# One image's lower-half columns moved from the prologue into layer 0, and what came with it: other DMA queues, a fourth tile of x, another source of a subtraction

## The chip, the cores and the metric

The kernel runs on one core of a Trainium2 chip. The metric is the device time of one execution in microseconds (us); less is better. Five engines work in parallel, each in its own order: TensorE (PE, with its weight loads as PEld), VectorE (DVE), ScalarE (ACT), GpSimd (POOL) and SyncE (SP), which here only issues DMAs. Data lie in DRAM, in SBUF (on chip, 128 partitions) or in PSUM (where TensorE writes its results).

## The reference

x has the shape 4 x 16 x 256 x 256 (images, channels, rows, columns). Two layers follow each other, each with a group norm ahead (8 groups of 2 channels) and a residual:

```
def _L0_conv_ref(x, conv_w, conv_b):          # on h = _gn(x)
    out = conv3x3(x, conv_w) + conv_b         # 16 -> 16*25 channels
    logits = out.reshape(N, C, 25, H, W)
    weights = softmax(logits, axis=2)
    return einsum('ncuij,ncuij->ncij', unfold5x5(x), weights)

x = x + _L0_conv_ref(_gn(x), conv_w, conv_b)
x = x + _L1_conv_ref(_gn(x), ...)             # silu and a cubic spline of 3x3 patches, as one convolution
```

So layer 0 computes 400 logits at each pixel, and with their softmax weighs the 25 neighbours of the normalized image, channel by channel. Layer 1 applies silu and spline bases to the normalized result and convolves them.

## The kernel before, in words

An image's 256 rows are two halves of 128 (NH = 2, "upper" is half 0). There are three stages.

*The prologue* (about the first 120 us). It loads all eight half images (`load_x`, L415 to L424): image 0 into `held`, which stays, the other six into a pool `xin` of three buffers, so that a load waits until the tile three earlier is done with. For every tile VectorE takes statistics (L534, L536), ScalarE squares it into `xq` (L543, one buffer), TensorE sums the squares (L546), and VectorE takes their maximum (L549), for a bound on the logits; the bound becomes the flag (L589) on which all engines branch (L1112, L1116) to layer 0. The weights of both layers are arranged too: `prepare0`, and `prepare1`, which also stores six small pieces of the silu weights on SP's queue (L513).

*The normalized image h in DRAM.* `normalize` (L264) writes h of one image in two layouts. Rows: ScalarE normalizes to `hsp` (L327), and `put_rows` stores it into `hs` (L288, SP's queue). Columns: ScalarE normalizes to `ht` (L340), TensorE transposes it into `tp`, a PSUM tile (L362), and three copies of the columns are made: `tt` (fp32), `hi` (its value rounded to fp32r) and `lo`, the rest, by a subtraction on VectorE (L370); `put_columns` stores `tt` into `hst` and `hi`, `lo` into `hsl` (L302, three stores of 260 KB for each half, SP's queue). Each column tile has a border element from the neighbouring half. h has 4 quarters of the channels (QC = 4) and 2 blocks of columns in each (QG = 4), so there are 8 blocks for each half.

`normalize` is a generator: each `next` issues a little. Its stores and loads are put off by so many steps (`moves`). For image 0 it is interleaved with the statistics of the other images in the prologue, with `tt` copied by VectorE. For images 1 to 3 it is stepped once in each step of layer 0 (`next(ahead, None)`), with `tt` copied by ScalarE; a block of columns takes six steps.

*Layer 0* (`layer0`, from about 120 to 2060 us). The order is image, half, strip of 32 columns (64 strips), and in a strip eight steps of 4 columns. In a step TensorE multiplies `am` (from `hst`) and `an` (from `hsl`) by the weights (L833, L837) into logits in PSUM; ScalarE takes the exponential into the first half of a tile `e` (L856); GpSimd multiplies it by `u`, rows of `hs`, into the second half (L861); VectorE adds up both, one step later (L700). `e` has four buffers. Once in a strip come the division on VectorE (L720 to L722, with the reciprocal `r` in PSUM) and the subtraction from x on GpSimd (L728). `am` and `an` are loaded two column groups (of two steps) ahead by SP (L648, L658), `u` by L672.

*Layer 1* (`layer1`, from about 2030 us): spline pieces on VectorE and ScalarE (L158 to L169), silu on ScalarE (L973), convolution on TensorE (L1037, L1047), and some copies on GpSimd (L1008, L1065, L1067).

What orders the work: each engine runs its list in the order that the framework's scheduler made in the prologue; in layers 0 and 1 the order is that of the program text (`in_order`). A DMA waits on its queue for what it needs and holds up what is behind it on that queue; a DMA on ScalarE's queue stands in ScalarE's own list.

Of the kernel before, what the change touches and what calls it, by code (L numbers as in the profile page):

```python
# [3 lines left out]

# [7 lines left out]
F32 = mybir.dt.float32  # L12
F32R = mybir.dt.float32r
AF = mybir.ActivationFunctionType
# [20 lines left out]
def conv_preact_kernel(  # L35
# [12 lines left out]
    nc = tc.nc  # L48
    B, C, H, W = x.shape
    G = 8  # L50
    GC = C // G
    P = 128
    NH = H // P
# [3 lines left out]
    PAD = K // 2  # L57
# [3 lines left out]
    SW = 32  # L61
# [199 lines left out]
                    hsl[b][h][:, :, w : w + RP].rearrange("c t r -> (c t) r"), zero[:, 0:RP],  # L261
                )

    def normalize(b, ptr, tiles, held=None, copier=None):  # L264

        prep, xps, tts, his, los = tiles
        copier = copier or nc.scalar.copy

        moves = [(20 + 4 * i, f) for i, f in enumerate(zeros(b, nc.sync))] if held is None else []

        def move():
            for f in [f for i, f in moves if i <= 0]:
                f()
            moves[:] = [(i - 1, f) for i, f in moves if i > 0]

        def load(q, h):
            if held is None and q < C // QC:
                nc.sync.dma_start(  # L280
                    xps[h][:, :, PAD : PAD + W],
                    x[b, q * QC : (q + 1) * QC, h * P : (h + 1) * P, :].rearrange(
                        "c p w -> p c w"),
                )

        def put_rows(q, h, hsp):
            r0 = PAD + h * P
            nc.sync.dma_start(  # L288
                hs[b][:, r0 : r0 + P, q * QC : (q + 1) * QC, :].rearrange(
                    "s r c w -> r s (c w)"),  # L290
                hsp.rearrange("p s c w -> p s (c w)"),
            )

        def put_columns(q, n):
            g0 = n * QG
            for h in range(NH):

                for to, ti, t in ((hst, 0, tts[n]), (hsl, 0, his[n]), (hsl, 1, los[n])):
                    d = to[b][h]
                    m = 2 if to is hsl else 1  # L300
                    t = t if t.dtype == F32 else t.bitcast(F32)
                    nc.sync.dma_start(  # L302
                        bass.AP(
                            tensor=d.tensor,
                            offset=d.offset + q * QC * m * CT + ti * CT + (1 + g0) * RP,
                            ap=[[QW * RP, W // QW], [m * CT, QC], [1, QG * RP]],
                        ),
                        t[:, h].rearrange("p g r -> p (g r)"),
                    )

        def border(t):
            nc.scalar.copy(t[:, 1, :, 0:1], t[:, 0, :, P : P + 1])
            nc.scalar.copy(t[:, 0, :, RP - 1 :], t[:, 1, :, 1:2])

        hts = {}

        def rows(q):
            for h in range(NH):
                xp = xps[h] if held is None else held[h][:, q * QC : (q + 1) * QC]
                hsp = prep.tile([P, NST, QC, SP], F32, name=f"hsp{b}_{q}_{h}", tag="hsp")  # L320
                ht = prep.tile([P, QW, W // QW, QC], F32, name=f"ht{b}_{q}_{h}", tag=f"ht{h}")
                hts[q, h] = ht
                for k in range(QC // GC):
                    g = q * (QC // GC) + k
                    kc = slice(k * GC, (k + 1) * GC)
                    how = dict(scale=nrm[b][:, 0, g : g + 1], bias=nrm[b][:, 1, g : g + 1])
                    nc.scalar.activation(  # L327
                        hsp[:, :, kc, :].rearrange("p s c w -> p c s w"),
                        bass.AP(
                            tensor=xp.tensor, offset=xp.offset + k * GC * (W + 2 * PAD),  # L330
                            ap=[xp.ap[0], [W + 2 * PAD, GC], [SW, NST], [1, SP]],
                        ),
                        AF.Identity, **how,
                    )
                    if k == QC // GC - 1:
                        nc.scalar.copy(hsp[:, 0, :, 0:PAD], zpad)
                        nc.scalar.copy(hsp[:, NST - 1, :, PAD + SW :], zpad)
                        moves.append((4, partial(put_rows, q, h, hsp)))
                    yield
                    nc.scalar.activation(  # L340
                        ht[:, :, :, kc].rearrange("p g w c -> p c w g"),
                        xp[:, kc, PAD : PAD + W].rearrange("p c (w g) -> p c w g", g=QW),
                        AF.Identity, **how,
                    )
                    if k == QC // GC - 1:
                        moves.append((4, partial(load, q + 1, h)))
                    yield

        def columns(q, n, h):

            tp = ptr.tile([P, QG, P], F32, name=f"tp{b}_{q}_{n}_{h}", tag="tp")

            def copy(t, to):

                to(t[:, h, :, 1 : 1 + P], tp)
                if h == 0:
                    to(t[:, 1, :, 0:1], tp[:, :, P - 1 :])
                else:
                    to(t[:, 0, :, RP - 1 :], tp[:, :, 0:1])

            for k in range(QG):
                nc.tensor.transpose(  # L362
                    tp[:, k, :], hts[q, h][:, n * QG + k].rearrange("p w c -> p (w c)"), ident
                )
            yield
            copy(tts[n], copier)
            copy(his[n], nc.scalar.copy)
            yield

            nc.vector.tensor_sub(  # L370
                los[n][:, h, :, 1 : 1 + P], tp, his[n][:, h, :, 1 : 1 + P].bitcast(F32)
            )
            if h == NH - 1:
                moves.append((5, partial(border, los[n])))
                moves.append((9, partial(put_columns, q, n)))
            yield
            yield
            yield
            yield

        for h in range(NH):
            load(0, h)
        yield
        for _ in rows(0):
            move()
            yield
        for q in range(C // QC):
            ahead = rows(q + 1) if q + 1 < C // QC else iter(())
            for n in range(QW // QG):
                for h in range(NH):  # L390
                    for k, _ in enumerate(columns(q, n, h)):
                        if k % 3 == 2:
                            next(ahead, None)
                        move()
                        yield
            for _ in ahead:
                move()
                yield
        while moves:
            move()  # L400
            yield


    with tc.tile_pool(name="prep0", bufs=2) as prep, tc.tile_pool(
        name="pre", bufs=1
    ) as pre, tc.tile_pool(
        name="xin", bufs=3
    ) as xin, tc.tile_pool(name="stat", bufs=2) as stat, tc.tile_pool(
        name="pstat", bufs=1, space=PSUM
    ) as pstat, tc.tile_pool(name="ptr0", bufs=3, space=PSUM) as ptr0:  # L410
# [30 lines left out]
            )  # L441
        for r in (4 * C, 6 * C):
            nc.sync.dma_start(wnr[r : r + 1, :], conv_b)
        nm = 3 * C
        sw = pre.tile([P, 3, 9, nm], F32, name="sw")
        ss = pre.tile([P, 3, 9, nm], F32, name="ss")
# [49 lines left out]
        def prepare1():  # L496
# [10 lines left out]
            for r in range(RT):  # L507
                nc.vector.tensor_copy(
                    wt[:, r : r + 3, :, r, :], wc.rearrange("p d (e o) -> p d e o", e=3)
                )  # L510
                for d in range(3):
                    p = SROWS.index(r + d) * C
                    nc.sync.dma_start(  # L513
                        ws[p : p + C, :, r, :],
                        wb1[d * C : (d + 1) * C].rearrange("p (e o) -> p e o", e=3),
                    )
# [9 lines left out]
        for b in range(B):  # L526
            st = stat.tile([P, G, NH * (GC if b == 0 else 1), 6], F32, name=f"st0_{b}", tag=f"st0{min(b, 1)}")
            for hf in range(NH):
# [19 lines left out]
                    )  # L548
                nc.vector.tensor_reduce(hm[:, n : n + 1], sq, AX.X, ALU.max)  # L549
                next(ahead, None)  # L550
                if n >= NH and n + 3 < B * NH:
                    loaded.append(load_x(n + 3))
            mean, rstd = group_stats(stat, pstat, st, f"x{b}")
            nc.vector.tensor_copy(nrm[b][:, 0], rstd)
            nc.vector.scalar_tensor_tensor(nrm[b][:, 1], mean, -1.0, rstd, ALU.mult, ALU.mult)
# [15 lines left out]
            if b == 1:  # L571
                prepare1()
            if b == 0:
                ahead = normalize(0, ptr0, tiles, held, nc.vector.tensor_copy)
                next(ahead)
        for _ in ahead:
            pass
# [42 lines left out]
    def layer0(shift):  # L620
# [4 lines left out]
        with tc.tile_pool(name=f"prep{arm}", bufs=2) as prep, tc.tile_pool(  # L625
# [172 lines left out]
            for n, (b, hf, s) in enumerate(strips):  # L798
                if (hf, s) == (0, 0):
                    for _ in ahead:  # L800
                        pass
                    ahead = normalize(b + 1, ptr, tiles) if b + 1 < B else iter(())
                    if b == B - 1:
                        bank = ptr.tile([P, QG, P], F32, name=f"ps{arm}", tag="tp")
                        first_scales = [scales(k, partial(lambda k: bank[:, k], k)) for k in range(2)]
                last = (hf, s) == (NH - 1, NST - 1)
                if last:
                    for _ in ahead:
                        pass
                u = us.pop(0)  # L810
                if s * SW % CX == 0:
# [350 lines left out]
```

## Time and profile before

| | |
|---|---|
| median of 3 runs | 3065.07 us (3059.95 to 3065.65) |
| the profiled execution | 3061.86 us, of it span 3059.8 us |
| VectorE busy | 2959.0 us, 97% |
| TensorE busy | 2802.6 us, 92% |
| ScalarE busy | 2236.6 us, 73% |
| GpSimd busy | 1947.6 us, 64% (until layer 1 begins, nearly all) |
| L861, GpSimd, e times u | 512 x 3.54 us |
| L700, VectorE, sums | 512 x 3.48 us |
| L370, VectorE, lo | 64 x 0.68 us: 16 in the prologue, 48 in layer 0 |
| L543, ScalarE, squares | 8 x 3.6 us |
| DMA, mean | 205 GB/s; 276 GB/s over the first 170 us |

How to read it: in a group's line stand the line of the code, the engine, the operation, what it writes and reads, how often, then the busy time and the mean duration, then the engine's idle time before it and what ended that. In a timeline's line stand start and duration. A following instruction's start may lie a little ahead of the end of the one before it on the same engine, so the time from start to start is shorter than the duration.

### The profile page before, as it was taken

Reading aid. Unit: us, or ns where it says so; the run is one execution under the profiler, and the core shown is the slowest. Engines: PE = TensorE matmul, PEld = TensorE weight load, DVE = VectorE, ACT = ScalarE, POOL = GpSimd, SP = SyncE. Lnnn points to the kernel's source line nnn. Section 1 sums busy time; section 2 is a strip of 40 time slices with the busy share of each in tenths; the row PEclk is TensorE's granted clock in tenths of the full one; section 3 lists DMA queues with packets and bytes.
Section 4 is the critical chain, followed back from the end, with each engine's and each line's share of the span. In section 5 each row is a group of like instructions: output and inputs, shape, how many; then the busy total and the mean of one; then the engine's idle time right before and its main releaser. Section 6 shows DMA issues by size and latency. Waiting matters only on the chain.

```text
span 3059.8 us, 39743 instructions
## 1 busy us (share of the span) xinstructions
PE 2802.6 (92%) x14248; PEld 1448.2 (47%) x14248; DVE 2959.0 (97%) x1587; ACT 2236.6 (73%) x2587; POOL 1947.6 (64%) x744
## 2 busy tenths in 40 slices
PE   4499999999999999999999999958999999999998
PEld 3366656656656666666666566632222222222222
DVE  7599999999999999999999999998999999999997
ACT  6466765676766566766646546559999999999996
POOL 4199999999999999999999999980100100000000
PEclk7699999999999999999999999978999999999999
DMA  8988977879878778978767667659999999999994
GB/s 273 290 223 221 258 205 209 222 189 257 234 209 240 196 202 225 248 216 220 212 174 200 164 173 194 161 131 198 201 192 195 198 194 189 198 194 202 190 197 91
DMA packets 350929, 626.29 MB, mean 205 GB/s; under 512 B 41330, under 2 KB 216676, under 8 KB 334852
## 3 DMA queue, kind: packets, MB, share of 16 engines
q1 hardware_dynamic: 318020, 605.29, 81.0%
q10 hardware_dynamic: 30960, 15.73, 1.8%
q0 software_dynamic: 1744, 2.64, 0.3%
q8 instruction: 117, 1.92, 0.3%
q14 instruction: 88, 0.72, 0.1%
HBM read 513.95 MB, written 104.24 MB: 202 GB/s over the span
## 4 chain that ended last, share of the span: by engine, by line
DVE 69%; issue 11%; PE 8%; DMA 3%; ACT 3%; POOL 2%; SPq 1%; DVEq 0%; ACTq 0%; POOLq 0%
DVE nd L700 44%; PE lg L833 6%; DVE ta L168 4%; DVE ta L167 4%; DVE tb L168 4%; DVE tb L167 4%; DVE tb L158 2%; PE lg L837 1%; DVE yo L1020 1%; POOL e L861 1%; DVE r L721 1%; DVE nd L720 1%; DVE lo L370 1%; DMA am<-hst 1%; DVE nd L722 1%
## 5 line engine op out<-in xcount | busy, mean ns | idle before, releaser
L861 POOL TENSOR_TENSOR e<-e,u 128x1600 f32<-128x1600 f32 x512 | 1788.4, 3539 | 49.0 <-ACT e L856 30.9
L833 PE MATMUL lg<-wm,am 128*128 128x400 f32 x4096 | 1734.8, 505 | 83.8 <-ACT e L856 53.0
L700 DVE TENSOR_REDUCE nd<-e 128x128 f32<-128x3200 f32 x512 | 1748.0, 3478 | 29.0 <-POOL e L861 28.9
L837 PE MATMUL lg<-wn,an 97*128 97x400 f32 x2048 | 1344.9, 657 | 17.3 <-DMA an<-hsl 17.3
L856 ACT ACTIVATE e<-lg 128x800 f32<-128x800 f32 x1024 | 818.2, 837 | 708.9 <-DVE nd L700 460.5
L833 PEld LDWEIGHTS lg<-wm,am 128*128 128x128 f32 x4096 | 760.9, 192 | 403.3 <-ACT e L856 98.2
L1037 PE MATMUL yp<-ring,wt 128*32 128x512 f32 x6144 | 745.9, 598 | 87.6 <-DVE ring L169 63.7
L837 PEld LDWEIGHTS lg<-wn,an 97*128 97x128 f32 x2048 | 388.3, 190 | 334.5 <-issue 23.6
L1037 PEld LDWEIGHTS yp<-ring,wt 128*32 128x32 f32 x6144 | 203.7, 109 | 621.7 <-issue 427.7
L954 POOL MEMSET sl<- 16x256 f32 x6 | 1.8, 306 | 402.7 <-ACT ta L163 299.8
L169 DVE SCALAR_TENSOR_TENSOR ring<-ta,ta 128x2048 f32<-128x2048 f32 (+1 forms) x64 | 147.9, 2310 | 2.5
L168 DVE TENSOR_TENSOR ta<-ta,ta 128x2048 f32<-128x2048 f32 (+1 forms) x64 | 147.5, 2305 | 2.8 <-ACT ta L166 2.8
L169 DVE SCALAR_TENSOR_TENSOR ring<-tb,tb 128x2048 f32<-128x2048 f32 x64 | 145.6, 2275 | 2.5
L748 ACT ACTIVATE z<-xc,nrm 128x256 f32<-128x256 f32 x240 | 144.2, 601 | 5.3 <-POOL xc L728 1.2
L168 DVE TENSOR_TENSOR tb<-tb,tb 128x2048 f32<-128x2048 f32 x64 | 145.4, 2271 | 0.0
L1047 PE MATMUL yp<-sl,ws 64*32 64x512 f32 (+1 forms) x1032 | 131.3, 602 | 0.0
L954 POOL MEMSET slc<- 16x256 f32 x2 | 0.6, 307 | 203.1 <-ACT ta L163 203.0
L166 ACT ACTIVATE ta<-ta 128x2048 f32<-128x2048 f32 (+1 forms) x64 | 123.4, 1928 | 2.0
L193 POOL TENSOR_TENSOR d<-d,nrz 128x8 f32<-128x8 f32 x4 | 2.7, 669 | 191.8 <-DVE d L191 191.8
L166 ACT ACTIVATE tb<-tb 128x2048 f32<-128x2048 f32 x64 | 120.6, 1884 | 0.0
L973 ACT ACTIVATE sl<-sl,q 64x2048 f32<-64x2048 f32 x43 | 90.0, 2094 | 1.1
L728 POOL TENSOR_TENSOR xc<-xc,nd 128x512 f32<-128x512 f32 x64 | 82.5, 1289 | 8.2 <-DVE nd L722 8.2
(195 smaller groups left out, 2089.3 us busy)
## 6 DMA issues: line engine op xcount, KB each, us to landing
am<-hst SPq DMA_DIRECT2D x512, 194.6 KB
u<-hs SPq DMA_DIRECT2D x320, 288.0 KB
an<-hsl SPq DMA_DIRECT2D x512, 129.8 KB
xta<-x1s SPq DMA_DIRECT2D x40, 1024.0 KB
xtb<-x1s SPq DMA_DIRECT2D x40, 1024.0 KB
xtc<-x1s SPq DMA_DIRECT2D x40, 1024.0 KB
am<-hst SPq DMA_DIRECT2D x256, 129.8 KB
sl<-x1s SPq DMA_DIRECT2D x166, 128.0 KB
```

Of the source, the lines that this page charges most:

```text
L166: nc.scalar.activation(s1, r1, AF.Square, scale=2.0)
L167: nc.vector.scalar_tensor_tensor(s2, t, 2.0, s2, ALU.subtract, ALU.mult)
L168: nc.vector.tensor_mul(s1, s1, r1)
L169: nc.vector.scalar_tensor_tensor(f, s2, 0.0, s1, ALU.min, ALU.subtract if given else ALU.add)
L700: nc.vector.tensor_reduce(nd[:, :, :, j : j + JG].rearrange("p t c j -> p t j c"), e.rearrange("p t j m c d -> p t j c m d"), AX.XY, ALU.add,)
L748: nc.scalar.activation(z, v, f, scale=nrm[b][:, 0, g : g + 1], bias=nrm[b][:, 1, g : g + 1], accum_out=st1[b][:, t, g, columns_of(n) : col ...
L833: nc.tensor.matmul(lg[:, i, :NL], lhsT=am[:, o : o + P], rhs=wm.rearrange("p m c d -> p (m c d)"), start=True, stop=False,)
L837: nc.tensor.matmul(lg[:, i, :NL], lhsT=an[:, o : o + P], rhs=wn.rearrange("p m c d -> p (m c d)"), start=False, stop=True,)
L856: nc.scalar.activation(ev, lg[:, :, :NL], AF.Exp)
L861: nc.gpsimd.tensor_tensor(e[:, 1].rearrange("p j m c d -> p j (m c) d"), e[:, 0].rearrange("p j m c d -> p j (m c) d"), uv, ALU.mult,)
L1037: nc.tensor.matmul(yp[t * M : (t + 1) * M], lhsT=wt[:, d, e].rearrange("p r o -> p (r o)"), rhs=ring[:, r0 + t * RT + d : r0 + t * RT + d ...
L1047: nc.tensor.matmul(yp[t * M : (t + 1) * M], lhsT=ws[v, e].rearrange("p r o -> p (r o)"), rhs=sl[n % 3][v, t : t + NT + 1 : NT, e : e + W], ...
```

## The change

- In the prologue `normalize` for image 0 gets `part = 0`: it still makes the rows of both halves and transposes both, but of the columns it copies and stores the upper half's alone. Of the lower half it takes the border element, and it keeps the upper half's border elements for later in three small tiles `kept`.
- The lower half's columns are made in layer 0: a second generator, `part = 1`, is chained ahead of image 1's. It loads the lower half of x again (`xp`, 4 loads), makes `ht` on ScalarE, transposes, makes `tt` and `hi` on ScalarE and `lo` on VectorE, and stores. It is finished by the strip numbered 6 at the latest; the lower half's columns are first read for strip 8.
- A block of columns takes four steps instead of six in this generator and in image 1's (`space = 1`).
- The subtraction that makes `lo` reads `tts[n]` (SBUF) where it read `tp` (PSUM), in all four images.
- In the prologue `put_rows` issues on ScalarE's queue instead of SP's, and one step after instead of four.
- The silu weights' six small stores are issued by GpSimd instead of SP.
- `xin` has four buffers instead of three, and the sixth tile of x is loaded ahead of the loop.

```diff
+    NQ = QW // QG
+    kept = [
+        const.tile([P, C // QC * NQ, QG, 1], d, name=f"kept{i}") for i, d in enumerate((F32, F32R, F32R))
+    ]
-    def normalize(b, ptr, tiles, held=None, copier=None):
+    def normalize(b, ptr, tiles, held=None, copier=None, part=None, space=3):
...
+        parts = range(NH) if part is None else (part,)
+        read = range(NH) if part != 1 else (1,)
...
-            nc.sync.dma_start(
+            (nc.sync if held is None else nc.scalar).dma_start(
                 hs[b][:, r0 : r0 + P, q * QC : (q + 1) * QC, :].rearrange(
...
-            for h in range(NH):
+            for h in parts:
 
                 for to, ti, t in ((hst, 0, tts[n]), (hsl, 0, his[n]), (hsl, 1, los[n])):
...
-                        moves.append((4, partial(put_rows, q, h, hsp)))
+                            moves.append((4 if held is None else 1, partial(put_rows, q, h, hsp)))
...
+                if h in parts:
+                    to(t[:, h, :, 1 : 1 + P], tp)
+                if part == 1:
+                    to(t[:, 1, :, 0:1], keep[:, q * NQ + n])
+                elif h == 1:
+                    to(t[:, 0, :, RP - 1 :], tp[:, :, 0:1])
                 else:
-                    to(t[:, 0, :, RP - 1 :], tp[:, :, 0:1])
+                    to(t[:, 1, :, 0:1] if part is None else keep[:, q * NQ + n], tp[:, :, P - 1 :])
...
-            copy(tts[n], copier)
-            copy(his[n], nc.scalar.copy)
+            copy(tts[n], copier, kept[0])
+            copy(his[n], nc.scalar.copy, kept[1])
             yield
+            v = slice(1, 1 + P) if h in parts else slice(RP - 1, RP)
+            to = h if h in parts else 0
             nc.vector.tensor_sub(
-                los[n][:, h, :, 1 : 1 + P], tp, his[n][:, h, :, 1 : 1 + P].bitcast(F32)
+                los[n][:, to, :, v], tts[n][:, to, :, v],
+                his[n][:, to, :, v].bitcast(F32),
             )
...
             yield
+            for _ in range(space):
+                yield
...
-        name="xin", bufs=3
+        name="xin", bufs=4
...
+        loaded.append(load_x(5))
...
-                    nc.sync.dma_start(
+                    nc.gpsimd.dma_start(
                         ws[p : p + C, :, r, :],
...
-                if n >= NH and n + 3 < B * NH:
-                    loaded.append(load_x(n + 3))
+                if n >= NH and n + 4 < B * NH:
+                    loaded.append(load_x(n + 4))
...
-                ahead = normalize(0, ptr0, tiles, held, nc.vector.tensor_copy)
+                ahead = normalize(0, ptr0, tiles, held, nc.vector.tensor_copy, 0)
...
-                    ahead = normalize(b + 1, ptr, tiles) if b + 1 < B else iter(())
+
+                    ahead = normalize(b + 1, ptr, tiles, space=3 if b else 1) if b + 1 < B else iter(())
+                    if b == 0:
+                        late = normalize(0, ptr, tiles, part=1, space=1)
+                        ahead = chain(late, ahead)
...
+                if n == NST - 2:
+                    for _ in late:
+                        pass
```

## The prediction, as it was put on record before the run

> **What bounds the kernel now.** I read the page first: busy shares, slices, chain of waits.
>
> ```profile
> PE 2802.6 (92%) x14248; PEld 1448.2 (47%) x14248; DVE 2959.0 (97%) x1587; ACT 2236.6 (73%) x2587; POOL 1947.6 (64%) x744
> ...
> DVE  7599999999999999999999999998999999999997
> ...
> DVE 69%; issue 11%; PE 8%; DMA 3%; ACT 3%; POOL 2%; SPq 1%; DVEq 0%; ACTq 0%; POOLq 0%
> ```
>
> VectorE (DVE) is full from the third slice (a slice is 76.5 us) to the end; only the first two, the prologue and the start of layer 0, have idle time. So anything that adds to VectorE's time in layer 0 (150 to 2040 us) adds to the total, and anything that shortens the prologue takes off it. Second, the groups of layer 0, in the stretch 160 to 640 us:
>
> ```profile
> L861 POOL TENSOR_TENSOR e<-e,u 128x1600 f32<-128x1600 f32 x131 | 457.7, 3548 | 7.8 <-ACT e L856 5.2 <-DVE nd L700 2.5
> L700 DVE TENSOR_REDUCE nd<-e 128x128 f32<-128x3200 f32 x130 | 444.2, 3478 | 1.0 <-POOL e L861 1.0
> L370 DVE TENSOR_TENSOR lo<-tp,hi 128x512 fp32r<-128x512 f32 x16 | 10.9, 681 | 0.0
> ```
>
> GpSimd (POOL) multiplies e by u almost without a pause (7.8 us idle in 480), VectorE reduces behind it (1.0 us idle). The third line is the subtraction that makes lo: 16 per image. Third, the timeline of one of them:
>
> ```profile
> 448.58 6.87 DVE L700 TENSOR_REDUCE nd<-e 128x128 f32<-128x3200 f32 x2
> 451.51 10.49 POOL L861 TENSOR_TENSOR e<-e,u 128x1600 f32<-128x1600 f32 x3
> ...
> 455.37 0.68 DVE L370 TENSOR_TENSOR lo<-tp,hi 128x512 fp32r<-128x512 f32 x1
> ...
> 455.96 6.87 DVE L700 TENSOR_REDUCE nd<-e 128x128 f32<-128x3200 f32 x2
> ```
>
> It starts in the middle of GpSimd's multiplications and still takes 0.68 us (0.60 from start to next start). One input, tp, lies in PSUM.
>
> Fourth, the one place where VectorE runs operations with two SBUF inputs (L167, L168, L169) while GpSimd reads SBUF, the start of layer 1:
>
> ```profile
> 2047.32 2.55 DVE L167 SCALAR_TENSOR_TENSOR ta<-xta,ta 128x2304 f32<-128x2304 f32 x1
> ...
> 2048.18 1.94 POOL L1065 COPY pad<-edge 128x258 f32<-128x258 f32 x1
> ...
> 2049.79 2.75 DVE L168 TENSOR_TENSOR ta<-ta,ta 128x2304 f32<-128x2304 f32 x1
> 2050.07 2.77 POOL L1067 COPY ring<-edge 128x50 f32<-128x50 f32 x2
> ...
> 2052.57 2.63 DVE L169 SCALAR_TENSOR_TENSOR ring<-ta,ta 128x2304 f32<-128x2304 f32 x1
> 2052.90 2.56 POOL L1008 COPY ring<-pad 128x258 f32<-128x258 f32 x1
> ```
>
> The copy of 128x258 takes 2.56 us here and 0.57 us at its fastest elsewhere (the minimum over L1008's four). L1065 ends at 2050.12, 0.25 us after L167 (2049.87); L1067 at 2052.84 after L168 (2052.54); L1008 at 2055.46 after L169 (2055.20). GpSimd's reads wait for the running VectorE operation and slip in at its end.
>
> [...] 0.68 us for lo beside a busy GpSimd (one SBUF input), 2.56 for 0.57 above. It shows GpSimd waiting for VectorE; the reverse order, VectorE behind a running multiplication, it doesn't show clearly. [...]
>
> **The change part by part.** The profiled execution took 3061.86 us (span 3059.8 and 2.1 around it), 3.2 below the median 3065.07.
>
> (1) *The source of the subtraction.* The diff turns `tp` (PSUM) into `tts[n]` (SBUF) in every call of the normalization; the second input, hi, is in SBUF too. In the built program's order layer 0 holds 56 of these: 3 images x 16 as before, and 8 of the lower half of image 0. All meet GpSimd's stream. For the 48 in the trace I took, at each one's start, what was left of the GpSimd operation then running: 0.05 to 3.51 us, mean 1.72. If VectorE waits for the end of that operation: 56 x 1.72 = +96.3 us. Queued behind it on VectorE are the next reductions; as VectorE has no idle time to give (2.7 us of waiting on GpSimd in all of layer 0), all counts. GpSimd loses 0.6 us per subtraction, 56 x 0.6 = 34 us, but it is the one ahead (two or three tiles of e at the subtraction), so this is hidden unless VectorE's wait is zero. Bounds: 0 (no contention) and 7.4 us each (VectorE gets in only when GpSimd has run out of tiles: the ring holds 4, the lead is 2.36 on average, so 1.72 + 1.64 x 3.485 us from start to start), 56 x 7.4 = 414 us. I take the waiter-gets-in-next reading, as GpSimd does in the last fence.
>
> (2) *Lower half's columns moved.* From the prologue go, per block, a copy on VectorE (0.60 from start to start), a copy on ScalarE (0.48), a subtraction (0.60), 3 stores of 260 KB on SP: eight times that. Layer 0 gets 8 subtractions: 8 x 0.60 = +4.8 us on VectorE. Its ScalarE work (8 ht of 1.1, 16 copies of 0.48, some 0.1 pieces: 20 us over 38 steps of 3.8 us), 32 transposes (0.11 each) and SP's 24 stores and 8 loads (about 0.6 each, 19 us over 145) lie beside engines with room: ScalarE 65% busy, SP issuing 3 us of am and an per 7.6. If that cover failed, a late am would show; bound 0 to 8 us, taken 0. The closer spacing for image 1 (subtractions every 4 reductions instead of 6) is the same work, earlier.
>
> (3) *The prologue's end.* ScalarE's list from 35.34 us on: 16 pairs of hsp and ht at 1.86 = 29.8, 5 squares of x at 3.52 = 17.6, 8 hi copies at 0.48 = 3.8, some 45 small ones at 0.1 = 4.5, weights 2.4: 58 us, so not before 93 without a wait. Before, it ended at 116.45, with 17 us of waits in the timeline. The rows' stores on its queue cost it 8 issues (0.40 each for L782's in layer 0, beside its work). SP loses its wait of 13.7 us at 59 us for hsp, during which the DMA engines fell idle; next late is then ScalarE itself. It meets new waits: its first store of h waits in the built program for the load of a weight (40 to 44 us), hsp buffers have to drain, and the last two squares stand behind everything, with the sum on TensorE between them (xq has one buffer, 3.4 us). Walking the built order of ScalarE, VectorE and SP with these durations, I get the last square to 110, its sum to 113.6, the flag to 116.6 (before: 113.4).
>
> ```profile
> 118.39 0.56 SPq L302 DMA_DIRECT2D hsl<-lo  x1
> 120.44 1.87 SPq L648 DMA_DIRECT2D am<-hst  x3
> ...
> 147.17 0.87 ACT L327 ACTIVATE hsp<-xp,nrm 128x576 f32<-128x576 f32 x1 [11.30 <-DMA am<-hst]
> ...
> 149.56 3.51 POOL L861 TENSOR_TENSOR e<-e,u 128x1600 f32<-128x1600 f32 x1 [9.21 <-ACT e L856]
> ```
>
> SP before issued its last store at 118.4 and the first am at 120.44; after, its stores are out early, and 1.5 us behind the flag gives 118.1: -2.3 us, bounds -15 (half of the waits vanish, x arrives earlier thanks to the fourth tile) and +5. The weights' six small stores (7 us of SP) go to GpSimd, at 0.5 us each (as L569), ahead of wm: about 1 us, hidden.
>
> (4) *Layer 0's start.* ScalarE stops at the first piece that needs xp until 147.17, after two steps' exponentials. In the new order three steps stand ahead of it: one GpSimd step more in the gap, -3.5 us; bounds -6 and 0.
>
> Sum: 96.3 + 4.8 - 2.3 - 3.5 = +95.3, so 3157.2 against the profiled run, 3160 against the median.
>
> **The rivals.** *No lock for this pair* [...]: then 4.8 - 2.3 - 3.5 = -1.0, 3064, not slower. It decides below 0.1 us per subtraction. For it: the trace never shows VectorE waiting like that in layer 0. Against: the fence of layer 1. With the prologue's bounds it spans 3048 to 3075. *Starving:* VectorE gets no turn inside a back-to-back stream: +414, about 3475. For it: L565 took 4.27 us at 37.33 (0.21 its other times) and ended with GpSimd's multiplication L498 at 41.6, having let several GpSimd instructions pass. Against: it is another kind of operation, and GpSimd does get in between VectorE's. *Half paid:* VectorE waits only for part of an operation, 0.5 to 1 us each, 28 to 56 us more than without the lock: 3092 to 3120.
>
> **How the numbers follow.** Forecast 0.50 (3125 to 3215), no lock 0.25 (of it 0.13 faster, 0.08 the same, 0.04 slower), starving 0.17, half paid 0.08. A measurement of this kernel tells about 0.2% (6 us). Faster 0.13, same 0.08, slower 0.79. From 3050 to 3220, starving is left out, and little else; the forecast's own range is 3125 to 3215.
>
> **What would show it.** lo's mean duration in layer 0 well over 0.68 us (about 2.4), ending with GpSimd's e; idle time of GpSimd rising by some 60 us; layer 0 longer by about 100 us while the sum of L700 stays. For step 3, the flag at 113 to 119 us; for step 4, three steps' multiplications ahead of the first ht. Wrong if lo stays at 0.68 us (then the prologue decides), or if it shows 7 us.

## The result, and the profile after

The changed kernel takes 3158.7 us (median of 4 runs, 3150.6 to 3165.9) against 3065.4 for the kernel before (median of 4, 3060.0 to 3069.9): ratio 1.030, 95% interval 1.027 to 1.034. The profiled execution, the fastest of the four, took 3150.6 us, of it span 3148.8: 89.0 more than the span before.

The page of the changed kernel, first: busy shares, the slices of VectorE, the shares of the chain of waits, and three groups (busy time and mean ns, then the idle time ahead and what ended it). L905, L737 and L395 are what was L861, L700 and L370; in the experiments these numbers shift by a line or two.

```profile
PE 2833.5 (90%) x14280; PEld 1460.4 (46%) x14280; DVE 3049.7 (97%) x1587; ACT 2246.2 (71%) x2619; POOL 1978.3 (63%) x750
...
DVE  7499999999999999999999999998999999999997
...
DVE 76%; issue 11%; DMA 4%; PE 3%; POOL 2%; ACT 2%; SPq 1%; DVEq 0%; POOLq 0%; ACTq 0%
...
L905 POOL TENSOR_TENSOR e<-e,u 128x1600 f32<-128x1600 f32 x512 | 1809.3, 3564 | 121.9 <-ACT e L900 95.1
L737 DVE TENSOR_REDUCE nd<-e 128x128 f32<-128x3200 f32 x512 | 1748.2, 3476 | 17.9 <-POOL e L905 17.9
...
L395 DVE TENSOR_TENSOR lo<-tt,hi 128x512 fp32r<-128x512 f32 x72 | 140.1, 1947 | 5.2 <-ACT hi L376 3.0
```

VectorE's share has not changed, 97%, yet it is busy 90.7 us longer. Its main work, the sums of L737, has not grown (1748.0 before). What has grown is the subtraction that makes lo: it did not stand among the costliest groups before and stands there now with 140.1 us. GpSimd's idle time ahead of e has risen from 49.0 to 121.9 us. So an instruction that does the same arithmetic "is busy" longer, while GpSimd, which had hardly a pause before, now has time to spare: VectorE's busy time here contains waiting that the profile counts as work.

The groups over layer 0 (160 to 2140 us), where all 56 of these subtractions lie:

```profile
L905 POOL TENSOR_TENSOR e<-e,u 128x1600 f32<-128x1600 f32 x505 | 1784.9, 3565 | 105.9 <-ACT e L900 91.2 <-ACT lo L404 6.7 <-DMA u<-hs 5.9
L737 DVE TENSOR_REDUCE nd<-e 128x128 f32<-128x3200 f32 x506 | 1727.2, 3476 | 1.0 <-POOL e L905 1.0
L395 DVE TENSOR_TENSOR lo<-tt,hi 128x512 fp32r<-128x512 f32 x56 | 133.4, 2383 | 0.0
```

2.38 us each where it was 0.68. In the prologue the eight full-size ones, from the same source, still take 0.67 to 0.69 us: no multiplication of e by u runs then. The timeline of one in layer 0 (start, duration, engine):

```profile
204.34 10.92 POOL L905 TENSOR_TENSOR e<-e,u 128x1600 f32<-128x1600 f32 x3
204.59 3.47 DVE L737 TENSOR_REDUCE nd<-e 128x128 f32<-128x3200 f32 x1
207.98 3.90 DVE L395 TENSOR_TENSOR lo<-tt,hi 128x512 fp32r<-128x512 f32 x1
211.81 6.87 DVE L737 TENSOR_REDUCE nd<-e 128x128 f32<-128x3200 f32 x2
```

GpSimd's second multiplication ends at 211.33 (its own record has 3.35 us left at 207.98); lo ends at 211.88, 0.55 us later, less than the 0.68 us that it takes alone. The third multiplication stands still in the meantime: it takes 3.96 us instead of 3.52, which is why the three take 10.92 and not 10.5.

The start of layer 0, in the timeline:

```profile
115.78 0.14 DVE L626 CAST flag<-bd 1x1 int32<-1x1 f32 x1
...
117.54 1.86 SPq L685 DMA_DIRECT2D am<-hst  x3
...
129.83 10.49 POOL L905 TENSOR_TENSOR e<-e,u 128x1600 f32<-128x1600 f32 x3 [12.14 <-DMA an<-hsl]
...
141.44 1.29 ACT L360 ACTIVATE ht<-xp,nrm 128x512 f32<-128x512 f32 x1 [4.83 <-DMA am<-hst]
...
144.18 17.47 POOL L905 TENSOR_TENSOR e<-e,u 128x1600 f32<-128x1600 f32 x5 [3.87 <-ACT e L900]
```

The flag is set at 115.78 (113.25 before), yet the first am is issued at 117.54 (120.44 before); three multiplications stand ahead of the wait for xp, and the next starts at 144.18, where before the third started at 149.56. (The profile names a load of am as what ended ScalarE's wait at 141.44; that the piece waits for xp is read from its operands.)

The account of the 89.0 us, from these two traces: the 56 subtractions wait 95.3 us in all (133.4 less 56 x 0.68); eight of them are new to layer 0, +4.8; the fourth sum of L737 starts at 147.74 instead of 157.03, -9.3. That makes +90.8; -1.8 remains, in small shifts inside layer 0 that I do not explain further. Layer 1 is the same (1012.5 us from the last sum to the end, 1012.4 before).

### The profile page after: what moved, and what is told of

The parts are those of the page before. It is cut to its first block, busy times and chain, and to the rows that moved or that the text cites. A ratio compares the mean times of both kernels' runs of the same rounds, so it can differ in the third digit from the quotient of the medians.

```text
span 3148.8 us, 39844 instructions
## 1 busy us (share of the span) xinstructions
PE 2833.5 (90%) x14280; PEld 1460.4 (46%) x14280; DVE 3049.7 (97%) x1587; ACT 2246.2 (71%) x2619; POOL 1978.3 (63%) x750
## 4 chain that ended last, share of the span: by engine, by line
DVE 76%; issue 11%; DMA 4%; PE 3%; POOL 2%; ACT 2%; SPq 1%; DVEq 0%; POOLq 0%; ACTq 0%
DVE nd L737 48%; DVE ta L169 4%; DVE ta L168 4%; DVE lo L395 4%; DVE tb L169 4%; DVE tb L168 4%; DVE tb L159 2%; POOL e L905 2%; PE lg L877 1%; DVE yo L1064 1%; DVE r L758 1%; DVE nd L757 1%; DVE nd L759 1%; DMA xin<-in_x_dram 1%; PE yp L1081 1%
## 5 line engine op out<-in xcount | busy, mean ns | idle before, releaser
L877 PE MATMUL lg<-wm,am 128*128 128x400 f32 x4096 | 1755.9, 510 | 147.8 <-ACT e L900 132.9
L905 POOL TENSOR_TENSOR e<-e,u 128x1600 f32<-128x1600 f32 x512 | 1809.3, 3564 | 121.9 <-ACT e L900 95.1
L737 DVE TENSOR_REDUCE nd<-e 128x128 f32<-128x3200 f32 x512 | 1748.2, 3476 | 17.9 <-POOL e L905 17.9
L900 ACT ACTIVATE e<-lg 128x800 f32<-128x800 f32 x1024 | 809.0, 836 | 789.7 <-DVE nd L737 648.5
L881 PEld LDWEIGHTS lg<-wn,an 97*128 97x128 f32 x2048 | 391.8, 191 | 325.3 <-issue 23.4
L395 DVE TENSOR_TENSOR lo<-tt,hi 128x512 fp32r<-128x512 f32 x72 | 140.1, 1947 | 5.2 <-ACT hi L376 3.0
```

Of the source, the lines that this page charges most:

```text
L395: nc.vector.tensor_sub(los[n][:, to, :, v], tts[n][:, to, :, v], his[n][:, to, :, v].bitcast(F32),)
L737: nc.vector.tensor_reduce(nd[:, :, :, j : j + JG].rearrange("p t c j -> p t j c"), e.rearrange("p t j m c d -> p t j c m d"), AX.XY, ALU.add,)
L877: nc.tensor.matmul(lg[:, i, :NL], lhsT=am[:, o : o + P], rhs=wm.rearrange("p m c d -> p (m c d)"), start=True, stop=False,)
L881: nc.tensor.matmul(lg[:, i, :NL], lhsT=an[:, o : o + P], rhs=wn.rearrange("p m c d -> p (m c d)"), start=False, stop=True,)
L900: nc.scalar.activation(ev, lg[:, :, :NL], AF.Exp)
L905: nc.gpsimd.tensor_tensor(e[:, 1].rearrange("p j m c d -> p j (m c) d"), e[:, 0].rearrange("p j m c d -> p j (m c) d"), uv, ALU.mult,)
```

## The experiments

**The theory**: a VectorE instruction with two SBUF inputs waits for the end of GpSimd's running multiplication, about 1.7 us each time, and this is the whole loss. **The first rival**: the moved work (stores, loads, closer spacing) costs it. **The second**: VectorE and GpSimd share their reads in proportion.

*1. The source undone.* The changed kernel with

```diff
-                los[n][:, to, :, v], tts[n][:, to, :, v],
+                los[n][:, to, :, v], tp if h in parts else tp[:, :, 0:1],
```

> The changed kernel with one edit undone: the subtraction that makes lo reads tp (PSUM) again, in all images. Theory (the subtraction with two SBUF inputs waits for the end of GpSimd's running multiplication, 1.71 us each, 56 of them in layer 0): 3158.7 - 56 x 1.71 = about 3063; with what the trace shows of the start (first am 2.9 us earlier, one more GpSimd step ahead) 3055 to 3064, lo back at 0.68 us in layer 0, GpSimd's idle time back near 50 us. Rival (the moved half is what costs: its stores, loads, closer spacing, ScalarE's work): stays at 3140 to 3160 with lo at 0.68 us and other waits ahead of L737.

Measured: 3063.0 us, ratio to the kernel before 1.0002 (0.9992 to 1.0013). The groups of its layer 0:

```profile
L905 POOL TENSOR_TENSOR e<-e,u 128x1600 f32<-128x1600 f32 x505 | 1764.2, 3547 | 39.0 <-ACT e L900 33.6 <-DMA u<-hs 5.1
...
L395 DVE TENSOR_TENSOR lo<-tp,hi 128x512 fp32r<-128x512 f32 x55 | 37.4, 680 | 0.0
```

0.68 us again, and GpSimd's idle time is down from 105.9 to 39.0 us. The first rival falls: all that was moved is still moved. One edit carries the whole loss, 3% of the time. The kernel lies at the upper end of what was expected, though: it is 8.8 us ahead of the kernel before at the tenth sum of layer 0 (169.68 against 178.49), and level with it at the last (2046.96 against 2047.40). 4.8 us of that go into the eight subtractions. Where the rest goes is not settled. One candidate is TensorE's waits from 150 to 700 us (in total, times, longest):

```profile
PE tp L385 <- DVE lo L395: 19.5, 11, 2.9
```

At four steps to a block the next block's transposes find tp, of which there is one buffer in layer 0, still unread by lo. The multiplications of am behind them are late, then the exponentials, then GpSimd: VectorE waits for it around 235, 415 and 450 us and loses 3.7 us between the 16th and the 128th sum (against the same sums of the kernel before, the added subtractions at 0.60 us apart). But TensorE's waits by themselves do not make this loss: in the four kernels of experiments 5, 7, 8 and 9, which have the same layer 0, TensorE waits 16.7 to 19.8 us for lo, and by the same count VectorE loses 1.1, 3.8, 6.9 and 1.4 us. In the changed kernel TensorE does not wait for lo, which leaves tp alone there; whether that saved any time, no run shows.

*2. The source alone.* The kernel before with

```diff
-                los[n][:, h, :, 1 : 1 + P], tp, his[n][:, h, :, 1 : 1 + P].bitcast(F32)
+                los[n][:, h, :, 1 : 1 + P], tts[n][:, h, :, 1 : 1 + P],
+                his[n][:, h, :, 1 : 1 + P].bitcast(F32),
```

> The kernel before with one edit: the subtraction reads tt (SBUF) in place of tp (PSUM), nothing is moved. Theory: 48 subtractions in layer 0 at 1.71 us more each, +82 us: 3147 (3135 to 3160), each about 2.4 us. Rival (the moved half costs, or both together): 3065, lo at 0.68 us.

Measured: 3159.8 us, ratio 1.0324 (1.0306 to 1.0342), +98 us for 48 subtractions:

```profile
L370 DVE TENSOR_TENSOR lo<-tt,hi 128x512 fp32r<-128x512 f32 x48 | 130.3, 2714 | 0.0
```

48 x (2.714 - 0.68) = 97.6: the waits account for the loss, well within its interval (94 to 105 us by the ratio). That is 16 us more than the 82 expected, and the time lies at the upper edge of the expected range. 35 of the 48 wait as in the excerpt from the changed kernel, for the rest of the running instruction (62 us in all, with the nine that hardly wait); four take 6.9 to 10.6 us and make up the other 35.5. One of the four:

```profile
734.83 13.96 POOL L862 TENSOR_TENSOR e<-e,u 128x1600 f32<-128x1600 f32 x4
...
740.17 10.38 DVE L370 TENSOR_TENSOR lo<-tt,hi 128x512 fp32r<-128x512 f32 x1
748.75 1.25 POOL L729 TENSOR_TENSOR xc<-xc,nd 128x512 f32<-128x512 f32 x1
...
755.69 3.52 POOL L862 TENSOR_TENSOR e<-e,u 128x1600 f32<-128x1600 f32 x1 [5.68 <-ACT e L857]
```

The multiplication that runs at 740.17 ends 1.67 us later; lo does not get in. Two more multiplications and L729 go by at their usual length; L729 ends at 750.00, GpSimd has nothing to do until 755.69, and lo ends at 750.55. All four end 0.55 us after the last GpSimd instruction ahead of a pause of over 5 us. The changed kernel has two like it (7.75 and 8.44 us, 14.8 us of its 95.3). So the forecast's picture, "gets in at the end of the running one", holds for most, and the starving that stood as a rival happens to a few. What decides which of the two it is, no run here shows.

*3. Twice as many turns.* The changed kernel with each subtraction in two halves:

```diff
-            nc.vector.tensor_sub(
-                los[n][:, to, :, v], tts[n][:, to, :, v],
-                his[n][:, to, :, v].bitcast(F32),
-            )
+            for g in (slice(0, QG // 2), slice(QG // 2, QG)):
+                nc.vector.tensor_sub(
+                    los[n][:, to, g, v], tts[n][:, to, g, v],
+                    his[n][:, to, g, v].bitcast(F32),
+                )
```

> The changed kernel with each subtraction in two of half the size (128x256), both from SBUF; the work is the same. Theory (turn by turn: who waits gets in at the end of the running operation, and holds it for one whole instruction): the first half waits 1.7 us; then GpSimd's next multiplication, which waits already, takes its turn, and the second half waits for all of it, 3.5 us: 56 x 3.5 = +196 over the changed kernel, 3355 (3300 to 3370; less if GpSimd sometimes runs out of tiles of e); the second halves take about 3.9 us. Rival (the two share the reads in proportion to the elements, or the wait is paid once for a pair that follow each other): 3158 to 3170, the second halves at 0.4 us.

Measured: 3283.4 us, ratio 1.0737 (1.0705 to 1.077): about 133 us over the changed kernel by the ratios, for the same number of elements (196 expected, and less if GpSimd runs out of tiles). The group and one pair:

```profile
L396 DVE TENSOR_TENSOR lo<-tt,hi 128x256 fp32r<-128x256 f32 x112 | 267.7, 2429 | 0.0
```

```profile
1324.20 4.22 DVE L396 TENSOR_TENSOR lo<-tt,hi 128x256 fp32r<-128x256 f32 x2
1324.43 7.38 POOL L906 TENSOR_TENSOR e<-e,u 128x1600 f32<-128x1600 f32 x2
```

Half the elements take as long as the whole did (2.43 against 2.38 us). In the pair the first half takes 0.56 us (it starts 0.28 us ahead of a multiplication's end), then the waiting multiplication has its turn, then the second half, 3.74 us. Of the 56 second halves 36 take 3.73 to 3.75, that is a whole multiplication and themselves (36 x 3.32 = 120 us); the other 20 take 0.41, 14 of them with GpSimd at a pause, to which it had come during the first half's wait. That is why it is 133 us and not 196. The proportional rival is out: the cost here goes by instruction (2.43 us for each half), not by element.

*4. A smaller dose.* The changed kernel with the SBUF source for image 2 alone (16 subtractions), tp elsewhere:

```diff
+                tts[n][:, to, :, v] if b == 2 or h not in parts else tp,
```

> The changed kernel with the SBUF source for image 2 alone (16 of the 56 subtractions of layer 0), tp for the others. Theory (a price for each, independent of the others): 16 x 1.71 = +27 over the kernel with tp everywhere, so about 3088 if that one takes 3061. Rival (the cost is a threshold: GpSimd loses its lead once and stays behind): either nothing or most of the 96 us.

Measured: 3096.7 us, ratio 1.0107 (1.0092 to 1.0123), 32 us over the first experiment (27 expected); the 16 wait 32.2 us, 12.8 of it in two that are passed over (9.42 and 4.76 us). The price goes with the number: 2.0 us for each of 16 here, 2.0 for each of 48, 1.7 for each of 56. No sign of a threshold between 16 and 56.

The next four runs take the rest of the change apart, all with lo from tp.

*5. The move alone*: the first experiment with the rows' stores and the weights' stores on SP's queue and three tiles of x, as before the change.

```diff
-            (nc.sync if held is None else nc.scalar).dma_start(
+            nc.sync.dma_start(
...
-                            moves.append((4 if held is None else 1, partial(put_rows, q, h, hsp)))
+                            moves.append((4, partial(put_rows, q, h, hsp)))
...
-        name="xin", bufs=4
+        name="xin", bufs=3
...
-        loaded.append(load_x(5))
...
-                    nc.gpsimd.dma_start(
+                    nc.sync.dma_start(
                         ws[p : p + C, :, r, :],
...
-                if n >= NH and n + 4 < B * NH:
-                    loaded.append(load_x(n + 4))
+                if n >= NH and n + 3 < B * NH:
+                    loaded.append(load_x(n + 3))
```

> The move of the lower half alone: lo from tp (PSUM), the rows' stores and the silu weights' stores on SP's queue again, three tiles of x. Theory (the queue edits free the prologue's end, worth some of the 8.8 us that the kernel with tp is ahead at the tenth reduction): first reductions later than in that kernel by 2 to 6 us, total 3065 to 3069. Rival (the eight blocks less alone shorten the start; the queue edits are hidden): 3061 to 3064, the same as with all edits.

*6. The queue edits alone*: the kernel before, with the lines that this diff takes away put in (its plus and minus the other way round).

> The kernel before with the queue edits alone: rows' stores on ScalarE's queue one step after, silu weights' stores by GpSimd, four tiles of x; the lower half stays in the prologue, lo from tp. Theory of the prediction's third step (SP's wait of 13.7 us for hsp goes, ScalarE's work sets the end): flag 0 to 3 us earlier than before's 113.3, SP's last column stores as late as ScalarE's last hi copies allow, total 3057 to 3063. Rival (the chain is set by x's arrival and the squares, nothing moves): 3061 to 3062.

*7. The move and the rows' stores on ScalarE's queue*: the first two of the diff's places as in the changed kernel, the others as before.

> The move of the lower half alone (lo from tp, as in the run that took 3049.4) plus one queue edit: rows' stores on ScalarE's queue, one step after. In the built program this pushes the squares of x back in ScalarE's list (the last from 80th to 108th place). Theory (this edit is what takes the gain of the move away): the last square at 105 to 108 us instead of 91, flag at 115 to 118 instead of 108.6, total 3058 to 3063. Rival (another of the three edits, or the DMA engines' load): 3047 to 3053, the last square near 91.

*8. The move and four tiles of x*: the places with `xin`, `load_x(5)` and `n + 4` as in the changed kernel, the others as before.

> The move alone (lo from tp) plus one other edit: four tiles of x. In the built program the squares come earlier in ScalarE's list (the last at the 73rd place instead of the 80th). Theory (the place of the squares in ScalarE's list sets the flag): last square at 85 to 91 us, flag 103 to 109, total 3044 to 3050. Rival (with one more x in flight the stores of h are late, and layer 0's first loads with them): 3050 to 3060.

Measured, ratio to the kernel before and its interval, with start times from one trace each (in us; layer 1, the same code in all kernels, takes between 1010 and 1022 us in the traces, so single traces differ by some us for other reasons too):

| kernel (lo from tp) | ratio | last square of x | flag | first am | 4th sum |
|---|---|---|---|---|---|
| before | 1 | 95.46 | 113.25 | 120.44 | 157.03 |
| queue edits alone | 1.0006 (0.9998 to 1.0014) | 110.24 | 119.86 | 121.06 | 157.28 |
| move alone | 0.9959 (0.9944 to 0.9973) | 91.09 | 108.58 | 109.83 | 141.78 |
| move, rows' stores | 1.0000 (0.9988 to 1.0013) | 107.43 | 117.59 | 119.30 | 149.81 |
| move, four tiles | 0.9965 (0.9952 to 0.9979) | 88.21 | 106.75 | 111.20 | 141.87 |
| move, all edits (exp. 1) | 1.0002 (0.9992 to 1.0013) | 107.48 | 117.44 | 119.18 | 148.53 |

My theory for experiment 5 is refuted in its sign: without the queue edits the start is 6.8 us earlier (fourth sum), not later, and so fast a time, 3049.4 us, neither theory had. Experiment 7 names the edit: the rows' stores on ScalarE's queue. The last square of x (L579), the flag and the first am in the timeline of the move alone:

```profile
91.09 3.62 ACT L579 ACTIVATE xq<-xin 128x4096 fp32r<-128x4096 f32 x1 [1.46 <-PE sq L582]
...
108.58 0.14 DVE L625 CAST flag<-bd 1x1 int32<-1x1 f32 x1
...
109.83 1.88 SPq L684 DMA_DIRECT2D am<-hst  x3
```

and with the rows' stores added:

```profile
107.43 3.62 ACT L579 ACTIVATE xq<-xin 128x4096 fp32r<-128x4096 f32 x1 [2.03 <-PE sq L582]
...
117.59 0.14 DVE L625 CAST flag<-bd 1x1 int32<-1x1 f32 x1
...
119.30 1.87 SPq L684 DMA_DIRECT2D am<-hst  x3
```

The eight issues themselves take 3.0 us of ScalarE's time. But the framework's scheduler, given stores in ScalarE's list, lays that list out anew. In the traces the last square is ScalarE's 83rd computing instruction in the move alone, and its 99th, with eight issues ahead of it too, with the rows' stores (the expectation's 80th and 108th place are counts in the built program). The longer list also waits more. From the first piece of h to the last square ScalarE takes 56.1 us in the one and 72.6 in the other, and of these it is idle 6.4 and 17.7 us. The largest part, 10.5 us in seven places (0.7 in one), is the small copy of a border element into `kept`, which stands in the list ahead of its time and waits for lo; another 2.9 us are pieces of `hsp` that wait for a rows' store to land. One line of each:

```profile
60.46 0.20 ACT L288 CAST kept<-lo 128x4 fp32r<-128x4 f32 x1 [3.03 <-DVE lo L395]
...
93.35 0.87 ACT L347 ACTIVATE hsp<-held,nrm 128x576 f32<-128x576 f32 x1 [1.88 <-DMA hs<-hsp]
```

Of the 16.3 us by which the last square is later, 9.0 reach the flag: in the move alone other work, TensorE's transposes and the statistics of the last image, stands between the two. With 9.5 us at the first am and 8.0 at the fourth sum this edit takes back most of the move's gain. By the ratios it costs 12.6 us; the rest comes up inside layer 0 (the last sums of the two traces lie 13.0 us apart), and no run takes that part apart. The time, 3064.4 us, is just above the 3058 to 3063 expected.

Experiment 6 has the time that was expected of it, 3062.9 us, but for another reason: alone, the edits push the last square from 95 to 110 us and the flag from 113 to 120, where I had it 0 to 3 us earlier. The first am moves by only 0.6 us, since in the kernel before SP's column stores, until 119 us, held it back and not the flag. Experiment 8, at 3053.1 us, is 3 us above its expected range though its flag is where it was expected: SP's last column store, at 109.11, is behind the flag there, so the first am follows the flag by 4.4 us (1.2 in the move alone), and the fourth sum is no earlier than in the move alone.

*9. All but the rows' stores*: the changed kernel with two edits undone, lo from tp and the rows' stores on SP.

> The changed kernel with two edits undone: lo from tp, rows' stores on SP's queue; the move, the silu weights' stores from GpSimd and four tiles of x stay. Theory: as the run with four tiles of x, with 6 stores (7 us of issuing) less on SP: 3043 to 3050, the fastest of all. Rival (SP was not what is waited for): the same as the run with four tiles to within 2 us.

Measured: 3047.9 us, ratio 0.9951 (0.9937 to 0.9965): the fastest of all, 0.5% under the kernel before and 3.4% under the changed kernel. Its fourth sum starts at 137.66 us, some 4 us ahead of the two runs that it is compared with; but in total time it is not told apart from the move alone (0.9959) and the move with four tiles (0.9965).

*10. Five steps for a block*, against TensorE's wait found in experiment 1: that kernel with

```diff
-                    ahead = normalize(b + 1, ptr, tiles, space=3 if b else 1) if b + 1 < B else iter(())
+                    ahead = normalize(b + 1, ptr, tiles, space=3 if b else 2) if b + 1 < B else iter(())
...
-                        late = normalize(0, ptr, tiles, part=1, space=1)
+                        late = normalize(0, ptr, tiles, part=1, space=2)
```

> The changed kernel with lo from tp, and with five steps for a block instead of four in image 0's lower half and in image 1. With four steps the trace shows TensorE waiting 19.5 us in 11 places for lo, which keeps tp's only bank, and VectorE 3.5 us further behind for it. Theory: those waits go, 3063 - 3.5 = 3059 to 3060 (before 3061.5 in the same call as that kernel). Rival (the waits of TensorE are hidden, and the 3.5 us come from somewhere else): 3063.

Measured: 3077.5 us, ratio 1.0061 (1.0042 to 1.0079), slower by 0.6%. It does not answer the question: five steps do not fit. The lower half's generator is not through by strip 6, nor image 1's by the end of image 0, and what is left is issued in one go. Against experiment 1 VectorE falls back 5.5 us between the 44th and the 52nd sum (strip 6 begins at the 48th) and 12.5 us between the 116th and the 124th (the last strip begins at the 120th). In between it gains 4.0 us on it, of which 1.8 are three subtractions that only come later. What experiment 1's 3.7 us come from stays open; that five steps leave too little time is shown.

*11. lo by TensorE and ScalarE* in layer 0 (in experiment 1's kernel, again with five steps):

```diff
...
+                tq = ptr.tile([P, QG, P], F32, name=f"tq{b}_{q}_{n}_{h}", tag="tp")
+                nc.tensor.matmul(
+                    tq, lhsT=minus, rhs=his[n][:, to, :, v], start=True, stop=False
+                )
+                for k in range(QG):
+                    nc.tensor.matmul(
+                        tq[:, k, :], lhsT=hts[q, h][:, n * QG + k].rearrange("p w c -> p (w c)"),
+                        rhs=ident, start=False, stop=k == QG - 1,
+                    )
+                yield
+                nc.scalar.copy(los[n][:, to, :, v], tq)
...
```

> In layer 0 lo is made by TensorE and ScalarE instead of VectorE: a second use of tp's bank takes (-1) x hi and adds the four transposes of h, and ScalarE copies the result to lo; blocks at five steps for image 0's half and image 1, six for the others; in the prologue lo is made from tp as before. The output is computed in another way. Theory (VectorE's list is what bounds layer 0, to the microsecond): 56 x 0.60 = 34 us less than the kernel with tp everywhere: 3063 - 34 = 3029 (3022 to 3040). Rival (TensorE, 92% busy, or ScalarE's place in line ahead of the exponentials becomes the bound, so that GpSimd gets e late): 3050 to 3080, with VectorE waiting for GpSimd.

Measured: 3085.5 us, ratio 1.0079 (1.0062 to 1.0096). The forced ends of experiment 10 are in it too (23.4 us behind the kernel before at the 124th sum). But in images 2 and 3, which have six steps, the 32 subtractions less should give 19 us, and it loses another 3. Its engines from 640 to 1600 us (length, busy time of PE, PEld, DVE, ACT and POOL with instructions, then clock, DMA share and GB/s):

```profile
640.00:1600.00 960.00, 945.48 (x3516) 628.53 (x3515) 940.11 (x354) 651.11 (x1124) 937.96 (x291) 0.99 0.81 220
```

TensorE is busy 945.5 of 960 us (917.6 before), VectorE 940.1 (956.9). The subtractions are off VectorE, and TensorE has hardly any time left: there were only 4% between the two. VectorE now waits 17.6 us for GpSimd's e in this stretch (0.8 before), as the rival said, and the time is even above its range, with the forced ends in it. What holds up e is TensorE: ScalarE's exponentials wait 253 us for its products in this stretch (124 before), while TensorE waits only 1.7 us for them (16.6 before).

## Why the prediction was right, point by point

- *What bounds the kernel*: right. In experiments 2 and 4 the waits of VectorE's subtractions (97.6 and 32.2 us) make up the whole change of time (98 and 32), in 3 they are 131 of 133.
- *Step 1, the source*: right in the sum, 95.3 us of waiting measured against 96.3, and right in the mechanism for most. The term is made up otherwise than I wrote: 54 subtractions wait 80.5 us (1.49 each, not 1.72), and two that GpSimd passes over add 14.8. In the kernel before, with the same edit, it is 62 + 35.5 for 48. The forecast took one of two readings where both occur: the wait for the running multiplication was a little shorter than assumed, the starving that was left out made up for it. So the closeness of this sum is luck in part, and so is that of the total, 3158.7 for 3160, where the four runs spread over 15 us. GpSimd's loss of 0.6 us each: about 0.45 for those multiplications that wait (3.96 to 3.98 instead of 3.52), hidden, as said; its idle time rose by 73 us, where I had put some 60.
- *Which engine waits*: that VectorE would wait behind a running multiplication was an estimate of mine; the trace of the kernel before showed clearly only the reverse order (a copy on GpSimd 2.56 us instead of 0.57). The trace of the changed kernel shows VectorE behind GpSimd (3.90 us instead of 0.68 at 207.98), and experiment 3 agrees: a full multiplication, 3.5 us, stands between two halves of 0.41 in 36 of 56 pairs. Of the two engines it is here mostly the one that waited that comes next, but not always (not for 2 of the 56 subtractions of the changed kernel).
- *Step 2, the moved columns*: +4.8 is confirmed by experiment 1, and the cover held in the changed kernel (TensorE does not wait for tp there). With lo from tp TensorE does wait at the closer spacing; I had not named it as a waiter for lo, though lo then holds tp's only buffer. What that costs stays open (experiment 1).
- *Step 3, the prologue's end*: the times are near, the flag's end at 115.9 (116.6 forecast), first am -2.9 us (-2.3). The attribution that goes with it was wrong. I wrote of SP's wait that it goes and of ScalarE that it "is next late" as if the queue edit were the price of a gain; in fact the move alone gives -10.6 and the rows' stores take +9.5 of it (single traces with lo from tp; the first am of the six kernels with the changed kernel's queues lies between 116.7 and 119.2). Walking the built order gave the sum because the loss was in that order; I did not walk the order of the parts by themselves, and so took for a gain what was a loss.
- *Step 4, layer 0's start*: -3.5 was too small, and the measured value lies just outside the bounds of -6 and 0. From the first am to the fourth sum it is 36.6 us before and 30.2 after, so -6.4: one more multiplication in the gap, as said, and the wait for xp ends 2.8 us earlier counted from the first am (141.44 - 117.54 against 147.17 - 120.44), which was left out.
- *The rivals*: no lock, that is no waiting of VectorE, out (0.68 to 2.38 us). Half paid, out: in experiment 3 the second half waits for a whole multiplication (3.73 to 3.75 us instead of 0.41) in 36 of 56 pairs. Starving: out as the rule, true for 2 of 56 (4 of 48, 2 of 16, 3 of 56 pairs in the other runs).

## What to carry to other kernels

When an operand moves between PSUM and SBUF, count the SBUF inputs of the VectorE instruction that reads it: with two, beside a GpSimd that streams from SBUF, each such instruction (a subtraction of 128x512) cost 1.7 to 2.0 us on average here, about half of a GpSimd instruction of 3.52 us, and cutting it in two made it dearer (133 us more for the 56). With one of the two in PSUM it took 0.68 us beside the same multiplications. So make such instructions few and large, or leave one input in PSUM. A DMA put on a computing engine's queue can cost more than its issue where a scheduler orders that list (here 12.6 us for 3.0 us of issuing): look at where the instructions that the critical path needs stand afterwards, and what the ones ahead of them wait for. Test the parts of a change apart: here one edit lost 3%, another lost the 0.4% that the move itself had won; without these two the change gains 0.5% instead of losing 3% (experiment 9).

## What the runs showed of the hardware that was not expected

- A VectorE instruction that waits for GpSimd this way does not always get its turn at the end of the running instruction. In 11 cases over four kernels two-input subtractions stayed behind one to three further GpSimd instructions, which ran at their usual length, and ended 0.55 us (0.28 for the halves) after the last one ahead of a pause of over 5 us in GpSimd's list. Why these, is open.
- The wait is booked as busy time of the waiting instruction on both engines: lo with 3.90 us for 0.68, e with 3.96 for 3.52. The view of waits shows none of it.
